# Splitting the product with v over three engines in a sparse graph attention kernel

## The chip, the cores and the metric

One core of a Trainium2 chip runs the kernel. The metric is the device time of one execution in microseconds (us), the median of several runs. Engines: PE is TensorE (PEld its weight loads), DVE is VectorE, ACT is ScalarE, POOL is GpSimd. SBUF is the core's working memory, PSUM the buffer that TensorE writes its results to. All runs compared here are in the fast state, and each kernel was timed beside runs of the kernel before on the same chip.

## The reference, cut to what matters

The task is one layer of graph attention with residuals and layer norms: 4096 nodes, 512 features, 8 heads of 64. The adjacency matrix is sparse, about 17 neighbours per node.

```python
q = (ht @ Wq + bq).reshape(T, H, HD) / sqrt(HD)
k = (hs @ Wk + bk).reshape(S, H, HD)
v = (hs @ Wv + bv).reshape(S, H, HD)
logits = einsum('thd,shd->hts', q, k)
logits = where(edge_mask[None] != 0, logits, NEG)
probs  = softmax(logits, axis=-1)
ctx    = einsum('hts,shd->thd', probs, v).reshape(T, D)
ht = layer_norm(ht + ctx @ Wo + bo)
out = _layernorm(x + ht + gelu(ht @ W1) @ W2)
```

## The kernel before: the parts that matter

The kernel makes lists of neighbours, projects k and v into a table in DRAM, and then treats targets in tiles of 128, sorted by their number of neighbours. Neighbours are called slots. GpSimd gathers the rows (k and v, 1024 floats) of three slots into one buffer. Six such buffers exist. VectorE multiplies k by q, reduces to logits, ScalarE exponentiates, VectorE multiplies v by the weights p, and TensorE transposes each product into one PSUM tile, where the transposes also sum over the slots. A feed-forward block (`pf`, `po`) is woven in between.

```python
def gather(dst, table, idx):
    nc.gpsimd.indirect_dma_start(out=dst, out_offset=None, in_=table[:, :], ...)   # L829

def values(i, j0, n, kv, p, cps, after):
    v4 = kv[:, :n, D:].rearrange("p j (h d) -> p j h d", h=H)
    nc.vector.tensor_tensor(v4, v4, p[:, j0:j0 + n, :].unsqueeze(3)                 # L942
                            .to_broadcast([P, n, H, HD]), ALU.mult)
    for j in range(n):
        for c in range(KC):
            nc.tensor.matmul(cps[:, c, :], kv[:, j, D + c * P:D + (c + 1) * P], ident,
                             is_transpose=True, ...)                                # L946
...
nc.vector.tensor_tensor(kv[:, :n, :D], kv[:, :n, :D],                               # L965
                        tq[:, :D].unsqueeze(1).to_broadcast([P, n, D]), ALU.mult)
nc.vector.tensor_reduce(lg[:, :n, :], ..., AX.X, ALU.add)                           # L969
nc.scalar.activation(p[:, j0:j0 + n, :], lg[:, :n, :], AF.Exp)                      # L973
...
if pend:
    values(*pend.pop())          # group k-1
    issue(k + AHEAD)             # three gathers, AHEAD = 4
```

`kv` and `tq` are in SBUF, `p` is in PSUM. The program order above is only a wish: a scheduler sets each engine's order when the program is built.

## Time and profile before

| | before |
|---|---|
| median (range) | 1908.8 us (1901.9 to 1910.5) |
| span of the profiled run | 1904.1 us |
| attention, first to last gather of k and v | 393 to 1766 us |
| TensorE, VectorE, ScalarE, GpSimd busy | 90, 84, 41, 50% |
| granted clock of TensorE | 0.970 |

The views are read in the prediction below: the busy table, the stretches, the groups by line, the queue of GpSimd. The shares are averages over stages.

### The profile page before, as it was taken

To read this page: it belongs to the slowest core of one execution; us is meant where nothing else is said; L and a number is where in the kernel's file an instruction comes from. 1 tells how busy PE (TensorE), PEld (TensorE's weight loads), DVE (VectorE), ACT (ScalarE), POOL (GpSimd) and SP (SyncE) were. 2 spreads that over 40 slices of the span, in tenths; PEclk is the share of its full clock that TensorE was granted. 3 is DMA by queue.
4 is the path that set the end of the run, shared out by engine and by line. 5 is a ranking of instruction groups with operands and counts; after the bars stand their busy time and mean duration, and the time that the engine had idled before them with its cause. 6 is when DMAs were issued, how large, how long until landed. Compare 5 with 4: busy or idle time off the path is not lost.

```text
span 1904.1 us, 21426 instructions
## 1 busy us (share of the span) xinstructions
PE 1722.6 (90%) x7282; PEld 1116.1 (59%) x7282; DVE 1597.0 (84%) x2845; ACT 772.7 (41%) x1234; POOL 958.0 (50%) x857
## 2 busy tenths in 40 slices
PE   6998889676889999997999999999999989899996
PEld 3443344333656666665676667666667666667664
DVE  5889987568999999998899899999999987788601
ACT  4666664432344455442343333343334333333310
POOL 1002332542544555566767676677766655556201
PEclk9999999898889999998999999999999999999998
DMA  8778875598988788876778787888888867677200
GB/s 288 253 242 269 284 261 190 182 359 307 381 293 290 263 287 285 284 239 200 252 258 302 238 315 262 311 270 301 298 292 290 276 224 259 212 252 256 81 1 24
DMA packets 145392, 482.34 MB, mean 253 GB/s; under 512 B 20292, under 2 KB 20856, under 8 KB 145272
## 3 DMA queue, kind: packets, MB, share of 16 engines
q0 software_dynamic: 99312, 356.83, 54.2%
q1 hardware_dynamic: 40256, 105.15, 16.7%
q10 hardware_dynamic: 5704, 18.89, 2.5%
q8 instruction: 60, 0.98, 0.2%
q14 instruction: 60, 0.49, 0.1%
HBM read 438.07 MB, written 42.73 MB: 253 GB/s over the span
## 4 chain that ended last, share of the span: by engine, by line
DVE 30%; PE 15%; DMA 12%; issue 9%; POOL 8%; ACT 1%; SPq 0%; DVEq 0%; POOLq 0%; ACTq 0%
DVE kv L965 9%; DMA kv<-kvd,rec 9%; DVE kv L942 7%; DVE lg L969 7%; PE po L1067 5%; POOL kv L829 5%; PE pf L1058 5%; PE cps L946 2%; PE t L899 2%; DMA w<-in_L_gnn_W_dram 2%; DVE cand L657 1%; DVE n_st L639 1%; DMA out_dram<-xt,rec 1%; DVE R L672 1%; POOL rec L729 1%
## 5 line engine op out<-in xcount | busy, mean ns | idle before, releaser
L829 POOL DMA_INDIRECT kv<-kvd,rec x600 | 707.3, 1179 | 382.4 <-PE cps L946 182.9
L1058 PE MATMUL pf<-h2T,w 128*128 128x256 f32 (+1 forms) x2176 | 475.0, 369 | 3.5 <-ACT h2T L926 2.9
L1067 PE MATMUL po<-w,gt 128*128 128x512 f32 x1024 | 468.6, 596 | 2.0 <-ACT gt L1061 2.0
L1058 PEld LDWEIGHTS pf<-h2T,w 128*128 128x128 f32 x2176 | 388.4, 192 | 73.5 <-issue 25.0
L965 DVE TENSOR_TENSOR kv<-kv,tq 128x1536 f32<-128x1536 f32 (+2 forms) x210 | 350.7, 1672 | 77.8 <-DMA kv<-kvd,rec 53.6
L942 DVE TENSOR_TENSOR kv<-kv,p 128x1536 f32<-128x1536 f32 (+2 forms) x210 | 349.4, 1667 | 3.5 <-ACT p L973 3.2
L969 DVE TENSOR_REDUCE lg<-kv 128x24 f32<-128x1536 f32 (+2 forms) x210 | 349.1, 1665 | 0.4
L946 PEld LDWEIGHTS cps<-ident,kv 128*128 128x128 f32 x2400 | 277.3, 143 | 91.4 <-DVE kv L942 45.7
L946 PE MATMUL cps<-ident,kv 128*128 128x128 f32 x2400 | 306.8, 277 | 24.5 <-DVE kv L942 23.6
L1067 PEld LDWEIGHTS po<-w,gt 128*128 128x128 f32 x1024 | 187.0, 192 | 184.0 <-issue 179.7
L629 POOL TENSOR_TENSOR n_rs<-n_ve,mhalf 128x2 f32<-128x2 f32 (+1 forms) x66 | 57.1, 865 | 330.0 <-DVE n_ve L622 290.1
L653 ACT ACTIVATE sg<-a 128x1024 uint8<-128x1024 int32 x128 | 135.1, 1056 | 184.6 <-DMA a<-in_adj_dram 118.5
L973 ACT ACT_TABLE_LOAD x83 | 106.5, 1283 | 164.7 <-DVE lg L969 142.0
L973 ACT ACTIVATE p<-lg 128x24 f32<-128x24 f32 (+2 forms) x178 | 34.3, 193 | 295.4 <-DVE lg L969 161.6
L1061 ACT ACTIVATE gt<-pf 128x512 f32<-128x512 f32 x128 | 76.5, 597 | 186.5 <-PE pf L1058 170.6
L899 PE MATMUL t<-wo,rb 128*128 128x512 f32 x256 | 124.7, 632 | 25.4 <-DVE rb L895 25.1
L1061 ACT ACT_TABLE_LOAD x110 | 141.1, 1283 | 2.0
L785 PE MATMUL pq<-wk,hT 128*128 128x512 f32 x256 | 118.9, 607 | 23.0 <-ACT row L787 18.7
L785 PE MATMUL pq<-wv,hT 128*128 128x512 f32 x256 | 116.9, 599 | 17.3 <-ACT row L787 8.7
L657 DVE MAX8 cand<-wd 128x8 uint16<-128x103 uint16 (+1 forms) x640 | 130.6, 251 | 0.7
L796 PE MATMUL pq<-wq,hT 128*128 128x512 f32 x256 | 118.3, 606 | 6.3 <-DVE row L799 4.5
L899 PEld LDWEIGHTS t<-wo,rb 128*128 128x128 f32 x256 | 49.8, 202 | 83.7 <-issue 52.3
(125 smaller groups left out, 1427.2 us busy)
## 6 DMA issues: line engine op xcount, KB each, us to landing
a<-in_adj_dram SPq DMA_DIRECT2D x128, 512.0 KB
kvd<-row ACTq DMA_DIRECT2D x32, 512.0 KB
kv<-kvd,rec POOLq DMA_INDIRECT x600
tq<-row SPq DMA_DIRECT2D x17, 512.0 KB
xin<-in_L_gnn_h_target_dram SPq DMA_DIRECT2D x16, 512.0 KB
w<-in_L_gnn_W_dram SPq DMA_DIRECT2D x8, 1024.0 KB
xin<-in_x_dram SPq DMA_DIRECT2D x15, 512.0 KB
tq<-row POOLq DMA_DIRECT2D x15, 512.0 KB
```

Of the source, the lines that this page charges most:

```text
L657: nc.vector.max(cand[:, h * SQ + s, :], wd[:, w0:w1])
L785: nc.tensor.matmul(pkv, hT[:, kc, j * P:(j + 1) * P], w[:, kc, :], start=kc == 0, stop=kc == KC - 1)
L829: nc.gpsimd.indirect_dma_start(out=dst, out_offset=None, in_=table[:, :], in_offset=bass.IndirectOffsetOnAxis(ap=idx, axis=0))
L899: nc.tensor.matmul(pa, ct[:, c, :], wo[:, c, :], start=c == 0, stop=c == KC - 1)
L942: nc.vector.tensor_tensor(v4, v4, p[:, j0:j0 + n, :].unsqueeze(3) .to_broadcast([P, n, H, HD]), ALU.mult)
L946: nc.tensor.matmul(cps[:, c, :], kv[:, j, D + c * P:D + (c + 1) * P], ident, is_transpose=True, start=j0 + j == 0 and c == 0, stop=j0 + j ...
L965: nc.vector.tensor_tensor(kv[:, :n, :D], kv[:, :n, :D], tq[:, :D].unsqueeze(1).to_broadcast([P, n, D]), ALU.mult)
L969: nc.vector.tensor_reduce(lg[:, :n, :], kv[:, :n, :D].rearrange("p j (h d) -> p j h d", h=H), AX.X, ALU.add)
L973: nc.scalar.activation(p[:, j0:j0 + n, :], lg[:, :n, :], AF.Exp)
L1058: nc.tensor.matmul(pf[:, k, :], w1[(f0 + k) // KC][:, kc, (f0 + k) % KC * P:((f0 + k) % KC + 1) * P], h2T[:, kc, :w], start=kc == 0, stop= ...
L1061: nc.scalar.activation(gt, pf, AF.Gelu_apprx_tanh)
L1067: nc.tensor.matmul(po[j], gt[:, k, j * P:(j + 1) * P], w2[(f0 + k) // KC][:, (f0 + k) % KC, :], start=False, stop=f0 + k == FC - 1, skip_g ...
```

## The change

The intent is to take work from the two fullest engines. In a group of three slots ScalarE makes the third product (eight products of 128x64, each with one weight per partition), so VectorE makes two. GpSimd adds the first two results, so TensorE transposes two results in place of three. Around this, a frame: gathers are issued earlier, the transposes are emitted one step later, the projections get a third PSUM buffer, and two flag tiles become 16-bit to make room.

```diff
-                        pkv = psi.tile([P, D], F32, name="pq", bufs=2)
+                        pkv = psi.tile([P, D], F32, name="pq", bufs=3)      # three places
...
+                    m = n - 1 if n == S else n
-                    v4 = kv[:, :n, D:]...; multiply by p[:, j0:j0 + n, :]
+                    v4 = kv[:, :m, D:]...; multiply by p[:, j0:j0 + m, :]
+                    slots = list(range(n))
+                    if m > 1:
+                        nc.gpsimd.tensor_add(kv[:, 0, D:], kv[:, 0, D:], kv[:, 1, D:])
+                        slots.remove(1)
+                    yield
-                    for j in range(n):
+                    for j in slots:            # transposes, as before
...
+                def by_scalar(kv, lg):
+                    pa = sp.tile([P, H], F32, name="pa")
+                    nc.scalar.activation(pa, lg[:, S - 1, :], AF.Exp)
+                    for hd in range(H):
+                        v = kv[:, S - 1, D + hd * HD:D + (hd + 1) * HD]
+                        nc.scalar.mul(v, v, pa[:, hd:hd + 1])
...
                             advance()
+                            if k:
+                                issue(k + AHEAD)
                             yield cost * n
                             if pend:
-                                values(*pend.pop())
-                                issue(k + AHEAD)
+                                tails.append(values(*pend.pop()))
...
+                            if n == S:
+                                by_scalar(kv, lg)
```

(Cut: the 16-bit flags, the closing condition of the transposes, the last call of `values`. "multiply by" stands for the `tensor_tensor` shown above. A *clump* below is a run of adds in GpSimd's queue with no gather between them.)

More of the change, by code (lines that the diff above doesn't have):

```diff
@@ L605, in late_constants @@
                 nc.vector.tensor_scalar_mul(bq8, bq8, HD ** -0.5)
-                pb = psi.tile([P, D], F32, name="pq", bufs=2)
+                pb = psi.tile([P, D], F32, name="pq", bufs=3)
                 for kc in range(KC):
@@ L674, in edges @@
                         nc.vector.match_replace(flat, top, flat, 0.0)
-                has = lp.tile([P, MAXE], F32, name="ehas")
+                has = lp.tile([P, MAXE], BF16, name="ehas")
                 nc.vector.tensor_scalar(has, rec[:, :MAXE], 0.0, 0.0, op0=ALU.is_gt,
@@ L793, in target @@
                     g, (t, hT) = order[n][1], state[n]
-                    pq = psi.tile([P, D], F32, name="pq", bufs=2)
+                    pq = psi.tile([P, D], F32, name="pq", bufs=3)
                     for kc in range(KC):
@@ L873, in finish @@
                 nc.vector.tensor_copy(degs[:, i:i + 1], rec[:, MAXE:MAXE + 1])
-                has = sp.tile([P, MAXE], F32, name="has", bufs=1)
+                has = sp.tile([P, MAXE], BF16, name="has", bufs=1)
                 nc.vector.tensor_scalar(has[:, :cap], rec[:, :cap], 0.0, None, op0=ALU.is_gt)
@@ L940, in values @@
                 def values(i, j0, n, kv, p, cps, after):
-                    v4 = kv[:, :n, D:].rearrange("p j (h d) -> p j h d", h=H)
-                    nc.vector.tensor_tensor(v4, v4, p[:, j0:j0 + n, :].unsqueeze(3)
-                                            .to_broadcast([P, n, H, HD]), ALU.mult)
-                    for j in range(n):
+                    m = n - 1 if n == S else n
+                    v4 = kv[:, :m, D:].rearrange("p j (h d) -> p j h d", h=H)
+                    nc.vector.tensor_tensor(v4, v4, p[:, j0:j0 + m, :].unsqueeze(3)
+                                            .to_broadcast([P, m, H, HD]), ALU.mult)
+                    slots = list(range(n))
[4 more added lines that the diff above has]
+                    for j in slots:
                         for c in range(KC):
@@ L947, in values @@
                                              is_transpose=True, start=j0 + j == 0 and c == 0,
-                                             stop=j0 + j == TILES[i][1] - 1, skip_group_check=True)
+                                             stop=j0 + n == TILES[i][1] and j == slots[-1],
+                                             skip_group_check=True)
                     if after is not None:
                         tails.append(after)
+                def by_scalar(kv, lg):
[4 more added lines that the diff above has]
+                        nc.scalar.mul(v, v, pa[:, hd:hd + 1])
                 for k in range(AHEAD + 1):
@@ L988, in attention @@
                             k += 1
-                values(*pend.pop())
+                tails.append(values(*pend.pop()))
                 while tails:
```

## The prediction

> **What bounds the kernel now.** I read the busy table and the slices first, then the groups by line and shape, then the waits, and last a table of stretches and the GpSimd queue in order of time.
>
> ```profile
> PE 1722.6 (90%) x7282; PEld 1116.1 (59%) x7282; DVE 1597.0 (84%) x2845; ACT 772.7 (41%) x1234; POOL 958.0 (50%) x857
> PE   6998889676889999997999999999999989899996
> DVE  5889987568999999998899899999999987788601
> ACT  4666664432344455442343333343334333333310
> POOL 1002332542544555566767676677766655556201
> ...
> DVE 30%; PE 15%; DMA 12%; issue 9%; POOL 8%; ACT 1%; SPq 0%; DVEq 0%; POOLq 0%; ACTq 0%
> ```
>
> Two engines share the bound, TensorE and VectorE: both are near full from slice 11 on, and the chain of waits jumps between them. ScalarE has more than half its time free. GpSimd looks half free, but that is an average: it is empty in the first eight slices and at 6 or 7 tenths in the middle. So I cut the run where the character changes (columns: PE, PEld, DVE, ACT, POOL busy us with counts, clock, DMA share, GB/s):
>
> ```profile
> 0.00:400.00 400.00, 339.10 (x929) 156.68 (x930) 309.84 (x1198) 226.01 (x413) 99.67 (x118) 0.98 0.74 248
> 400.00:900.00 500.00, 443.33 (x1967) 298.82 (x1966) 473.33 (x830) 207.16 (x324) 270.72 (x237) 0.94 0.81 290
> 900.00:1100.00 200.00, 190.80 (x904) 135.90 (x903) 179.12 (x175) 74.53 (x109) 136.38 (x115) 0.99 0.77 261
> 1100.00:1500.00 400.00, 380.66 (x1824) 269.92 (x1823) 380.71 (x341) 148.05 (x217) 288.73 (x242) 0.98 0.86 295
> 1500.00:1770.00 270.00, 254.58 (x1167) 178.16 (x1165) 223.23 (x218) 97.26 (x141) 151.16 (x135) 0.98 0.72 242
> ```
>
> Attention runs from 393 us (first gather of k and v) to 1766 us (last). At 1100 to 1500 us VectorE and TensorE are both at 95%. The groups that the change touches, in the whole run and in that stretch (busy us, mean ns, then idle before and its releasers):
>
> ```profile
> L829 POOL DMA_INDIRECT kv<-kvd,rec x600 | 707.3, 1179 | 382.4 <-PE cps L946 182.9 <-issue 150.8 <-DVE lg L969 14.4
> L942 DVE TENSOR_TENSOR kv<-kv,p 128x1536 f32<-128x1536 f32 x189 | 329.3, 1743 | 3.5 <-ACT p L973 3.2 <-issue 0.3
> L946 PE MATMUL cps<-ident,kv 128*128 128x128 f32 x2400 | 306.8, 277 | 24.5 <-DVE kv L942 23.6 <-issue 0.4
> ...
> L829 POOL DMA_INDIRECT kv<-kvd,rec x208 | 255.4, 1228 | 87.9 <-issue 53.1 <-PE cps L946 26.3 <-remote 3.0
> ```
>
> Each gather is followed by 0.30 us in which GpSimd waits for nothing that the profile shows. That is queue time, though not counted as busy. The gathers in order of time show it, with the first VectorE product, which has two SBUF inputs, beside them:
>
> ```profile
> 1206.39 0.94 POOL L829 DMA_INDIRECT kv<-kvd,rec  x1 [0.30 <-issue]
> 1207.63 0.94 POOL L829 DMA_INDIRECT kv<-kvd,rec  x1 [0.31 <-issue]
> 1208.87 2.20 POOL L829 DMA_INDIRECT kv<-kvd,rec  x1 [0.30 <-issue]
> ...
> 1208.51 1.75 DVE L965 TENSOR_TENSOR kv<-kv,tq 128x1536 f32<-128x1536 f32 x1
> ```
>
> A free gather takes 1.24 us from start to start. One that meets the product with q takes 2.20 us and ends as soon as that product has ended plus the usual time. Over all gathers, those that overlap this product average 1.59 us and the others 0.95 us.
>
> **What the Trainium skill says.** "SBUF — State Buffer", section "SBUF: two separate sides": VectorE with two SBUF inputs and GpSimd share a port pair as "an exclusive lock, not a bandwidth split". The gathers above behave so beside the product with q. The product with p does not hold gathers up (1.21 us against 1.16), and its second input lies in PSUM. The new add on GpSimd reads SBUF, so it can block, and be blocked by, the product with q.
>
> "GPSIMD Engine Reference", section 3.1 "Elementwise": an elementwise op with two tensors costs about twice what VectorE takes. The trace agrees. This kernel already runs 128x512 f32 products on GpSimd (1.27 us, undisturbed) and on VectorE (0.687 us).
>
> "ScalarE: Activation LUTs", section "What ACT_TABLE_LOAD costs": a table load takes about 1283 ns, and an activation some 186 ns + 0.833 ns per element, with 93 ns for each pointer operand, partly hidden back to back. The trace has 1283 ns loads and 194 ns for 128x24. With that page I estimate 0.24 us for one of the new 128x64 products, whose scale is a pointer.
>
> **The change part by part.** There are 210 groups of slots: 189 of three, 12 of two, 9 of one.
>
> VectorE: the product with p shrinks from 128x1536 (1743 ns) to 128x1024 (1208 ns, from the twelve groups of two): 189 x 0.535 = 101 us less.
>
> TensorE: 189 + 12 = 201 groups have one result less to transpose, so 201 x 4 = 804 transposes go. The mean of 277 ns is a modelled span of overlapping instructions. In order of time twelve of them cover 1.47 us, and eleven weight loads 1.23 us, so one costs 0.11 us of the queue: 88 us less.
>
> ScalarE: 189 x (one exponential 0.19 + 8 products x 0.24) = about 400 us more, from 773 to about 1170 us. It stays the least loaded engine, 66 to 70% in the stretch at 1100 us (37% + 17 groups per 100 us x 2.1 us). The built order has only six more table-load rows, counting both branches. The products start from the same logits as the exponential before them, so they run beside the next VectorE work. A gelu may wait up to 2 us behind them, which two buffers for its result mostly hide.
>
> GpSimd: 201 adds of 1.27 + 0.08 us (the gap seen between two such products) = 271 us more, plus what the lock costs: the product with q is on for 1.75 us of about 6.5 us per group, so every fourth add waits about 0.9 us, 0.2 us each. I use 1.55 us per add. The adds stand in the same queue as the gathers. In the built order they come in clumps of one to four, mostly three, after up to nine gathers, because six buffers allow that. Buffers are freed only after the add and its transposes.
>
> Third PSUM buffer for projections: before 450 us TensorE waits for ScalarE or VectorE to empty such a buffer for about 40 us. But the start of attention also hangs on the edge lists, on VectorE (91% at 100 to 300 us) and on the adjacency rows. I give it 8 us. The 16-bit flags make room in SBUF and are worth nothing here.
>
> Now the sum by stretch, with groups = gathers / 3 and queue time = busy + gaps of 0.3 us.
> - 0 to 400: -8 us.
> - 400 to 900, 63 groups: VectorE bound, saves 63 x 0.535 = 34; TensorE saves 63 x 0.44 = 28. GpSimd has 271 + 67 of 500 us; with 63 x 1.55 it comes to 436 and still fits. -28 us.
> - 900 to 1100, 30 groups: GpSimd 136 + 33 = 169, plus 46 = 215 in 200 us. +10 us, with some of the overrun met by lower lock time.
> - 1100 to 1500, 69 groups: 289 + 70 = 359, plus 107 = 466 us in 400. VectorE would need only 381 - 37 = 344, TensorE 381 - 30 = 351. GpSimd becomes the bound: +55 us, a little under the full 66 because a longer stretch meets fewer blocks.
> - 1500 to 1770, 37 groups: 151 + 40 + 57 = 248 of 270; TensorE could save 16. Two engines near full in lockstep: -8 us.
> - From 1770 on only the feed-forward runs: 0.
> The sum is +21 us on the 1909.5 us median: 1930 us. About 190 us of work leave the two bounding engines, and nearly all of the gain is spent on a new bound.
>
> **The rivals.** First, the plain reading: two engines share the bound, both lose about 5% of the run, and the helpers are free on average. Then 80 to 90 us go, and the time is near 1825 to 1850. For it speak the busy table and the idle time of GpSimd, much of which is a wait for the transposes that get fewer (183 us). Against it: in the stretch at 1100 us only 26 us of that wait are left in 400.
>
> Second, the clumps hurt more than the sum says. Until now a gather waited for TensorE alone. After the change GpSimd also stands still until VectorE has made the products, gathers behind it are late, and TensorE waits in order for the adds in front of feed-forward work. One more microsecond for each of 201 groups makes 2000 us or more. Six buffers and nine gathers per clump (11 to 14 us against about 15 us of VectorE work in three groups) speak against the worst.
>
> Third, ScalarE delays gelu and through it TensorE: at 70% load in one in-order queue I expect tens of short waits, 10 us in all.
>
> **Range and chances.** The first rival pulls down by up to 100 us and the second up by 70, so I take 1868 to 1995 us for 8 in 10. Within 2% means 1871 to 1948 us. Faster 0.22, same 0.46, slower 0.32.
>
> **What would show it.** Right: the VectorE product at about 1.2 us, transposes down to 1596, an add row on GpSimd with 201 entries of 1.3 to 1.6 us, and at the middle of attention GpSimd busy above 80% while VectorE and TensorE drop to 80 to 88%, with waits for gathers before the product with q well above today's 54 us. Groups would come every 6.5 us or slower there against 5.8 today. Wrong: if GpSimd shows room in the middle (gathers quicker than 1.2 us, or adds under 1 us), the first rival holds; if VectorE falls under 75% there, or TensorE waits long for the adds, the second.

## The result, and the profile after

The changed kernel takes 2038.6 us (2037.2 to 2046.7, 4 runs) against 1908.8 us. The ratio is 1.0696 (95% interval 1.0658 to 1.0735). A ratio here is the mean time of one kernel's fast runs over that of the other's in the same rounds, so it isn't quite the ratio of the medians. It is slower by 7%, above the range of the prediction.

The busy line of the changed kernel:

```profile
PE 1699.4 (83%) x6478; PEld 1068.1 (52%) x6478; DVE 1610.6 (79%) x2845; ACT 1177.8 (58%) x2941; POOL 1226.2 (60%) x1058
```

TensorE lost its 804 transposes, ScalarE and GpSimd took their new work as planned (1178 and 1226 us). But VectorE is *not* less busy: 1611 us against 1597, though its product with p shrank. The groups show where most of its saving went (busy us, mean ns, idle before and its releasers; by shape). First a line of the kernel before, then the changed kernel:

```profile
L965 DVE TENSOR_TENSOR kv<-kv,tq 128x1536 f32<-128x1536 f32 x189 | 330.2, 1748 | 74.8 <-DMA kv<-kvd,rec 50.7 <-PE pf L1058 12.2 <-DMA tq<-tq,rec 6.8
...
L981 DVE TENSOR_TENSOR kv<-kv,tq 128x1536 f32<-128x1536 f32 x189 | 390.9, 2069 | 169.2 <-DMA kv<-kvd,rec 148.9 <-issue 9.9 <-DMA tq<-tq,rec 4.8
...
L949 POOL TENSOR_TENSOR kv<-kv 128x512 f32<-128x512 f32 x201 | 263.8, 1327 | 111.1 <-DVE kv L945 108.2 <-DVE n_nm L634 0.4 <-issue 0.4
L945 DVE TENSOR_TENSOR kv<-kv,p 128x1024 f32<-128x1024 f32 x201 | 242.6, 1209 | 15.0 <-ACT p L989 12.9 <-ACT kv L966 1.3 <-issue 0.6
L954 PE MATMUL cps<-ident,kv 128*128 128x128 f32 x1596 | 235.3, 297 | 123.6 <-POOL kv L949 122.2
```

The product with p costs 1.21 us, as worked out. The product with q, which the change doesn't touch, went from 1748 to 2069 ns on the mean. And there are three new waits: GpSimd's add for VectorE's product (108 us), TensorE's transposes for the add (122 us), and VectorE for gathers (149 us here, 51 us before). Their sum isn't the loss, since they overlap and lie partly off the path.

One place in order of time shows the first of these. The queue of GpSimd, then VectorE:

```profile
1316.46 3.73 POOL L949 TENSOR_TENSOR kv<-kv 128x512 f32<-128x512 f32 x3
...
1317.55 4.26 DVE L981 TENSOR_TENSOR kv<-kv,tq 128x1536 f32<-128x1536 f32 x1
```

Three adds run back to back to 1320.19 us. The product with q starts among them and ends at 1321.81, which is 1.62 us after the last add: about its whole time alone. It stood still through the clump. I compared start and end of every product of 128x1536 with every add in the trace: the 57 that overlapped an add averaged 2.81 us (4.73 us the longest), the 132 others 1.75 us. That is 57 x 1.06 = 60 us of VectorE standing, recorded as busy, and the same as the difference of the two lines above (390.9 - 330.2).

The product with q is not all. VectorE's other instructions that overlap an add took 35 us longer in sum than their medians in no_add (a run below, without the add), the smaller products with q 5 us. For example, a product of 16-bit tiles, `wd`, took 1.08 us where it overlapped an add (11 times) and 0.45 us elsewhere; `xt`, normalised in place, took 1.80 us (7 times) and 0.54 us elsewhere. So VectorE stands for about 100 us, as much as it was to save.

The stretches (columns as in the prediction):

```profile
400.00:900.00 500.00, 408.14 (x1676) 269.70 (x1676) 460.55 (x815) 319.12 (x812) 338.33 (x280) 0.90 0.80 283
900.00:1100.00 200.00, 167.40 (x667) 112.03 (x666) 159.03 (x155) 119.80 (x329) 154.69 (x134) 0.90 0.66 226
1100.00:1500.00 400.00, 326.23 (x1342) 224.00 (x1340) 331.38 (x288) 247.43 (x684) 312.89 (x256) 0.91 0.70 243
```

In the middle TensorE is at 82% and VectorE at 83%: no engine is full by this view. GpSimd comes nearest, at 78% busy plus some 13% of gaps. The windows do not hold the same work in both kernels, so I also timed the same gathers, counted from 1 to 600, from start to start (single rows move by up to 10 us if the count is shifted by one, since gathers come in bursts):

| work (gathers of k and v) | before | after | difference | predicted |
|---|---|---|---|---|
| until the first | 393 us | 394 us | +1 | -8 |
| 1 to 194 (ends at 900 us before) | 507.5 | 532.6 | +25 | -28 |
| 194 to 283 (1100) | 200.3 | 215.5 | +15 | +10 |
| 283 to 490 (1500) | 399.6 | 483.9 | +84 | +55 |
| 490 to the last (1766) | 265.2 | 271.2 | +6 | -8 |

The loss is everywhere in attention, and largest where GpSimd is fullest.

### The profile page after: what moved, and what is told of

It is laid out like the page before. It is cut to its first block, busy times and chain, and to the rows that moved or that the text cites. A ratio compares the mean times of both kernels' runs of the same rounds, so it can differ in the third digit from the quotient of the medians.

```text
span 2036.5 us, 22105 instructions
## 1 busy us (share of the span) xinstructions
PE 1699.4 (83%) x6478; PEld 1068.1 (52%) x6478; DVE 1610.6 (79%) x2845; ACT 1177.8 (58%) x2941; POOL 1226.2 (60%) x1058
## 5 line engine op out<-in xcount | busy, mean ns | idle before, releaser
L829 POOL DMA_INDIRECT kv<-kvd,rec x600 | 690.9, 1151 | 248.8 <-issue 170.0
L981 DVE TENSOR_TENSOR kv<-kv,tq 128x1536 f32<-128x1536 f32 (+2 forms) x210 | 416.4, 1983 | 180.5 <-DMA kv<-kvd,rec 160.2
L1086 PE MATMUL po<-w,gt 128*128 128x512 f32 x1024 | 480.1, 607 | 6.0 <-ACT gt L1080 5.6
L1077 PEld LDWEIGHTS pf<-h2T,w 128*128 128x128 f32 x2176 | 397.1, 195 | 78.1 <-issue 29.6
L966 ACT ACTIVATE kv<-kv,pa 128x64 f32<-128x64 f32 x1512 | 389.4, 335 | 10.4 <-issue 0.4
L954 PE MATMUL cps<-ident,kv 128*128 128x128 f32 x1596 | 235.3, 297 | 123.6 <-POOL kv L949 122.2
L949 POOL TENSOR_TENSOR kv<-kv 128x512 f32<-128x512 f32 x201 | 263.8, 1327 | 111.1 <-DVE kv L945 108.2
L954 PEld LDWEIGHTS cps<-ident,kv 128*128 128x128 f32 x1596 | 202.7, 153 | 186.5 <-POOL kv L949 154.2
L945 DVE TENSOR_TENSOR kv<-kv,p 128x1024 f32<-128x1024 f32 (+1 forms) x210 | 248.5, 1186 | 15.0 <-ACT p L989 12.9
L899 PE MATMUL t<-wo,rb 128*128 128x512 f32 x256 | 136.3, 682 | 48.2 <-DVE rb L895 48.2
```

Of the source, the lines that this page charges most:

```text
L899: nc.tensor.matmul(pa, ct[:, c, :], wo[:, c, :], start=c == 0, stop=c == KC - 1)
L945: nc.vector.tensor_tensor(v4, v4, p[:, j0:j0 + m, :].unsqueeze(3) .to_broadcast([P, m, H, HD]), ALU.mult)
L949: nc.gpsimd.tensor_add(kv[:, 0, D:], kv[:, 0, D:], kv[:, 1, D:])
L966: nc.scalar.mul(v, v, pa[:, hd:hd + 1])
L981: nc.vector.tensor_tensor(kv[:, :n, :D], kv[:, :n, :D], tq[:, :D].unsqueeze(1).to_broadcast([P, n, D]), ALU.mult)
L1077: nc.tensor.matmul(pf[:, k, :], w1[(f0 + k) // KC][:, kc, (f0 + k) % KC * P:((f0 + k) % KC + 1) * P], h2T[:, kc, :w], start=kc == 0, stop= ...
```

## The experiments

My theories when I began: *queue length* (GpSimd has too much to do per group, the main step of the prediction), *coupling* (VectorE, GpSimd and TensorE wait for each other in fixed order), *port lock* (the add and the product with q exclude each other), and *ScalarE* (its products delay others). Twelve kernels ran, each in 3 timed rounds.

| run | what | median us | ratio to before |
|---|---|---|---|
| change | all | 2038.6 | 1.0696 |
| no_add | without the add | 1942.2 | 1.0167 |
| frame | frame only | 1925.0 | 1.0079 |
| add_early | add on finished data | 2004.3 | 1.0494 |
| spread_add | add behind the newest gathers | 2174.0 | 1.1399 |
| no_scalar | without ScalarE's product | 2057.6 | 1.0754 |
| add_vec | add on VectorE | 1910.5 | 1.0000 |
| set_early | fill on finished data | 1895.2 | 0.9915 |
| spread_early | add ahead of its step's gathers | 1994.6 | 1.0434 |
| set_late | fill in the add's place | 1962.8 | 1.0273 |
| se_set | spread_early with a fill | 1915.1 | 1.0042 |
| third_buf | third PSUM buffer alone | 1905.7 | 0.9992 |
| vec_old | add on VectorE, old frame | 1903.2 | 0.9976 |

**1. Take parts away: no_add, no_scalar, frame, third_buf.**

```diff
 no_add
-                    if m > 1:
-                        nc.gpsimd.tensor_add(kv[:, 0, D:], kv[:, 0, D:], kv[:, 1, D:])
-                        slots.remove(1)
 no_scalar
-                    m = n - 1 if n == S else n
+                    m = n
-                            if n == S:
-                                by_scalar(kv, lg)
 frame: both;  third_buf: the kernel before with bufs=3 for "pq"
```

> The changed kernel without the add on GpSimd: ScalarE still takes the third product, VectorE the other two, TensorE transposes all three results again (2400 transposes). If the add on GpSimd is the whole cost (by its queue time, its order or the shared port), the time falls below the kernel before, to 1850 to 1900 us, since VectorE keeps its 101 us of saving and GpSimd is as free as before. If the ScalarE products (390 us of them) or the new program frame are a large part of the loss, it stays above 1960 us.

> The changed kernel without ScalarE's product: VectorE makes all three products, GpSimd still adds two results, TensorE transposes two. If the add on GpSimd is the main cost, 2000 to 2070 us, as slow as the whole change. If ScalarE's 390 us of products are a main cost, it falls below 1980 us.

> Only the frame of the change: third PSUM buffer, 16-bit flags, gathers issued earlier, transposes emitted one step later; VectorE makes all three products, no add, no ScalarE product. All theories: within 1.5% of the kernel before (1880 to 1935 us), by the third buffer perhaps 8 us faster. If it is above 1950 us, the frame itself costs and the others are to be read anew.

> The kernel before with the third PSUM buffer for projections alone. I predicted 8 us of gain from it: 1895 to 1908 us. If it is the part of the frame that costs (frame 1925 us): 1918 to 1930 us.

Without the add 96 us of the 130 are gone; without ScalarE's product none. So the add is the main cost and ScalarE isn't. But no_add missed my figure by 42 us: it is slower than the kernel before, and 17 us slower than the frame alone, although VectorE is busy far less. Its busy line:

```profile
PE 1736.5 (89%) x7282; PEld 1134.0 (58%) x7282; DVE 1507.9 (78%) x2845; ACT 1176.5 (61%) x2941; POOL 935.4 (48%) x857
```

VectorE fell by 89 us and the time did not fall. TensorE still has its 7282 operations. So moving a third of VectorE's product to ScalarE bought nothing here by itself; why it costs 17 us on top of the frame stays open. The frame costs 16 us. Its third buffer alone made no difference (1905.7 us): that leaves the new order of emission and the 16-bit flags, which I did not part.

**2. The same queue time without the waits: add_early.** The add works on the halves with k times q, which are done a group earlier and which TensorE doesn't read. Its output is wrong, which doesn't matter for the time.

```diff
-                        nc.gpsimd.tensor_add(kv[:, 0, D:], kv[:, 0, D:], kv[:, 1, D:])
+                        nc.gpsimd.tensor_add(kv[:, 0, :D], kv[:, 0, :D], kv[:, 1, :D])
```

> Wrong result on purpose: the same add of the same size on GpSimd, but on the halves that hold k times q, which are finished a group earlier and which TensorE does not read. Queue time, port lock and release of buffers stay; the waits of the add for the product with p and of the transposes for the add go. Theory of coupling (waits in order between VectorE, GpSimd and TensorE): falls by more than 80 us, to 1900 to 1955 us. Theory of queue length (GpSimd simply has too much to do per group): stays at 2000 to 2040 us. Theory of the port lock alone: stays as well.

It fell by 34 us only. At 2004.3 us it lies at the edge of what queue length and lock had been given (2000 to 2040 us) and far from the figure of the coupling (1900 to 1955): the waits between product, add and transposes are a part, but most of the loss is still there.

**3. The same queue time without reading SBUF: set_early and set_late.** GpSimd fills 1359 floats with zero in place of the add. That takes 1.25 us and only writes. In set_early it stands where add_early's add stood, in set_late where the change's add stood, with the same waits. Their outputs are wrong, which doesn't matter for the times.

```diff
 set_early
+                        nc.gpsimd.memset(kv[:, :n, :453 if n == S else D], 0.0)
 set_late
+                        nc.gpsimd.memset(kv.rearrange("p j d -> p (j d)")[:, D:D + (1359 if n == S else 2 * D)], 0.0)
```

> Wrong result on purpose, as add_early, but in place of the add GpSimd fills 1359 elements with zero, which takes about the same 1.27 us (from the fills at the start of the program) and reads nothing from SBUF. Against add_early at 2004 us: theory of the port lock between an add that reads SBUF and the product with q: the product goes back from 2.01 us to about 1.75 us and the time falls by 40 to 60 us, to 1945 to 1965 us. Theory of queue time: within 15 us of 2004 us.

> Wrong result on purpose: the fill of 1359 zeros (1.25 us, reads nothing from SBUF) stands exactly where the add stood, on the two slots that it joined, so it waits for the product with p and the transposes wait for it. Only the reading of SBUF is gone. Theory of the port lock: 1900 to 1945 us, against 2039 us with the add. Theory of queue time or of waits in order: above 2000 us.

set_early is 109 us faster than add_early, about twice the gain that I expected of the lock, and even 0.85% faster than the kernel before. set_late is 76 us faster than the change and 18 us above my range for the lock. The groups in add_early, then in set_early:

```profile
L981 DVE TENSOR_TENSOR kv<-kv,tq 128x1536 f32<-128x1536 f32 x189 | 380.3, 2012 | 136.2 <-DMA kv<-kvd,rec 116.0 <-PE pf L1077 9.2 <-DMA tq<-tq,rec 4.5
L949 POOL TENSOR_TENSOR kv<-kv 128x512 f32<-128x512 f32 x201 | 271.4, 1365 | 76.7 <-DVE lg L985 74.4 <-DVE n_nm L634 0.3
```

```profile
L981 DVE TENSOR_TENSOR kv<-kv,tq 128x1536 f32<-128x1536 f32 x189 | 331.1, 1752 | 61.0 <-DMA kv<-kvd,rec 45.4 <-DMA tq<-tq,rec 6.2 <-PE pf L1077 3.5
L949 POOL MEMSET kv<- 128x1359 f32 x189 | 232.8, 1252 | 34.4 <-DVE lg L985 34.3
L949 POOL MEMSET kv<- 128x1024 f32 x12 | 11.6, 970 | 0.0
```

The product with q is back at 1.75 us, whether it overlaps a fill (55 products, 1.753 us) or not (134, 1.752 us); in add_early the 46 that overlapped an add took 2.83 us, up to 5.95. With it the wait for gathers before that product falls from 116 to 45 us. GpSimd's busy time for adds or fills differs by only 27 us (271.4 against 232.8 + 11.6), less than the 109. So most of it is the lock, not the queue.

A fill holds VectorE up too. VectorE's instructions other than the product with q that overlap a fill took 43 us longer in sum than their medians in no_add: `xt` 1.94 us (7 times) against 0.57 us, while `wd` is not held (0.45 and 0.46 us). So these pairs measure the reading of SBUF, and not all that VectorE and GpSimd do to each other.

There was one flaw: the order of clumps in GpSimd's queue differs between fill and add in both pairs (add_early has 6 clumps of three and 7 of four, set_early one of each).

**4. Hold the order fixed: spread_add, spread_early, se_set.** An ordering edge puts each add behind the newest group of gathers (spread_add), or behind the group before and ahead of its own step's gathers (spread_early). In both, the queue alternates three gathers and one add. se_set is spread_early with the fill.

```diff
 spread_add
-                        nc.gpsimd.tensor_add(...)
+                        with tc.issue_after(newest[0].ins):      # last gather issued
+                            nc.gpsimd.tensor_add(...)
 spread_early: besides, issue(k + AHEAD) moves behind values(...), and
+                    with tc.issue_after(newest[1].ins):          # last add
+                        newest[0] = gather(...)
 se_set: spread_early with set_late's fill as the add
```

> The changed kernel with one ordering edge: each add is queued behind the newest gather of its own program step, so that GpSimd's queue alternates three gathers, one add, in place of clumps of two to four adds. All work is the same. Theory of coupling by clumps: the waits of GpSimd for the product with p (108 us) mostly go, time 1930 to 1990 us. Theory of queue length: within 20 us of 2039 us.

> As spread_add, three gathers and one add in turn, but each add stands one group of gathers earlier, in front of the gathers of its own step. In spread_add each add was stuck behind gathers that wait for a buffer which the add before it had to set free: a loop without slack. Theory of that loop: 1990 to 2060 us, far below 2174 us. If alternation as such is bad: above 2120 us.

> Wrong result on purpose: spread_early with the same fill in place of the add, so that GpSimd's queue is held to the same fixed alternation of gathers and fills in both, and a different order of clumps can't be the reason. Port lock: falls by 60 us or more from 1995 us, to 1890 to 1935 us, and the product with q from 2.11 us to about 1.75 us. If the gain of set_early came from its other order: within 20 us of 1995 us.

spread_add was a clear miss: I expected a gain and it lost 135 us more, with GpSimd's wait for the product almost gone as planned. Its waits (us in total, times, longest):

```profile
PEld cps L955 <- POOL kv L950: 384.4, 172, 11.0
DVE kv L982 <- DMA kv<-kvd,rec: 288.7, 133, 5.2
PE cps L955 <- POOL kv L950: 286.4, 144, 10.8
...
POOL kv L829 <- PE cps L955: 171.6, 76, 7.0
```

TensorE waits for adds at 144 places, and gathers wait for transposes. The add stands behind gathers that need the buffer which the add before it has to set free through TensorE: a ring without slack over six buffers. Moved ahead by one group of gathers, the same work takes 179 us less (spread_early, 1994.6 us, the best order that I found with the add on GpSimd). The clumps of the change lie between these two, so the change's order is not the worst one, which is what I had thought.

With the alternation held the same, the fill in place of the add gains 79 us (1994.6 to 1915.1), and the product with q goes from 2.11 to 1.75 us:

```profile
L983 DVE TENSOR_TENSOR kv<-kv,tq 128x1536 f32<-128x1536 f32 x189 | 398.0, 2106 | 141.4 <-DMA kv<-kvd,rec 124.7 <-issue 6.2 <-PE cps L956 5.2
```

```profile
L983 DVE TENSOR_TENSOR kv<-kv,tq 128x1536 f32<-128x1536 f32 x189 | 331.3, 1753 | 125.4 <-DMA kv<-kvd,rec 89.1 <-PE cps L956 13.2 <-issue 8.4
```

Of the 79 us, 67 are the standing of this product itself (398.0 - 331.3). The granted clock of TensorE is the same in both (0.937 and 0.935). The other engines' orders were still the scheduler's, and the fill is about 0.1 us shorter than the add (1.25 against 1.37 us, some of which is the lock again). Three pairs now agree on 76 to 109 us for an add that reads SBUF.

**5. Take the add off GpSimd: add_vec, vec_old.** `nc.vector.tensor_add` in place of `nc.gpsimd.tensor_add`, in the new frame and in the frame of the kernel before.

> The add moves from GpSimd to VectorE (201 adds of about 0.69 us, so VectorE does some 37 us more than in the kernel before); TensorE keeps its 804 transposes less; GpSimd is as free as before. If it is GpSimd's queue that costs, 1880 to 1935 us. If any further step between the product and the transposes costs, wherever it runs, above 1960 us.

> In the frame of the kernel before (two PSUM buffers, gathers issued behind the product, transposes with it): ScalarE takes the third product, VectorE the other two and their add, TensorE transposes two. add_vec without the new frame. If the frame costs 16 us here as well, 1885 to 1900 us, which would beat both kernels; if the split of work gains nothing, 1905 to 1925 us.

add_vec is as fast as the kernel before, 128 us faster than the change, although VectorE does 136 us of adds. vec_old is 1903.2 us, between its two expected ranges, ratio 0.9976 with interval 0.9934 to 1.0018: no proven gain. So the rearrangement is worth nothing with the add on VectorE, the one form with fewer transposes, a right result and no add on GpSimd that I ran; the fastest correct kernels here (vec_old, third_buf, before) can't be told apart.

## Why the prediction was wrong

**Most parts were sized right.** The product with p at 1.21 us, 1596 transposes, 201 adds at 1.33 us (1.3 to 1.6 predicted), ScalarE at 1178 us (1170; its 1512 products cover 389.4 us, 0.26 us each, where the estimate from the skill's page was 0.24), TensorE and VectorE at 82 and 83% in the middle (80 to 88). GpSimd was at 78% there, just under the sign of "above 80%".

**The step that failed** is the cost of the lock in "The change part by part": "every fourth add waits about 0.9 us, 0.2 us each". I had seen the lock and named it, but counted only one side, the add that waits for the product. The other side is dearer: the product with q, on one of the two fullest engines, stands still for the add, and through a whole clump of adds. Instead of 201 x 0.2 = 40 us on GpSimd the runs show 76 us (set_late), 79 us (se_set) and 109 us (set_early) of time for the same edit, reading SBUF or not. Directly it is 60 us of VectorE standing in the product with q, and 40 us in its smaller forms and in other instructions, which the prediction did not have at all; the rest is argued, not shown: VectorE's delay makes the next add, transposes and gathers late. With the reading alone taken out (set_late, 1963 us) the time is inside the predicted range, 33 us above its figure.

**The queue step was partly right.** GpSimd did become full: in set_early, where the product with q isn't held and most waits are gone, busy time plus gaps fill about 97% of GpSimd between 900 and 1500 us. The same gathers 283 to 490 take 435.4 us there against 399.6 before: +36 us, where I had put +55. That the queue causes this is not shown: in add_vec, without any add in GpSimd's queue, the same gathers take 429.7 us, +30 (there VectorE has the adds). And the queue alone isn't the loss, for set_early as a whole beats the kernel before.

**The light stretches.** I booked 36 us of gain in the first and the last stretch of attention by comparing loads with the length of each stretch. Set against the table above, -28 and -8 became +25 and +6. set_early shows what was there without most of the lock and the waits: 11, 4 and 22 us gained in the three stretches beside the middle. A sum of loads that "still fits" isn't yet a time when three engines wait for each other in order.

**The rivals.** The second rival (clumps and waits) was real and had too little weight: 34 us (add_early against the change) to 68 us (set_early against set_late). With the lock it carries the time to where it is. The first rival, the plain reading, found no support: VectorE's 89 us less gave nothing (no_add), and with both engines relieved and no reading of SBUF 14 us were gained (set_early), not 80 to 90, though GpSimd's fills take queue time there. The third, ScalarE, isn't the cause of the loss: without it the kernel is 19 us slower still.

**The third buffer**, -8 us, was 0 (third_buf: 1905.7 against 1908.7 us, interval of the ratio 0.9966 to 1.0018).

**Slips in the working** that did not decide it: GpSimd isn't empty in the first eight slices but 25% busy (99.67 of 400 us); 37% + 17 x 2.1% is 73% for ScalarE, not 66 to 70 (62% was measured); the first rival's 80 to 90 us lead to 1820 to 1830, not 1825 to 1850 us; the result of gelu has three buffers in the kernel, not two; a held gather ends 0.8 us after the product, a little less than the whole 0.94 us of a free one; and 1909.5 us is one run, the median is 1908.8.

A ledger from the medians, along one path of edits: before 1909; frame +16; ScalarE's product +17 (no_add less frame); fewer transposes, paid with a fill's queue time, -47 (set_early less no_add); reading SBUF +109 (add_early less set_early); waits in order +34 (change less add_early): 2038. By the other path, over set_late, the waits are 68 and the reading 76. Each edit is built in its own order by the scheduler, so single terms carry an error of about the 34 us by which the two paths differ. The granted clock of TensorE was lower after (0.922 against 0.970); in add_vec and set_early it was 0.940 too, and their times are at or below the time before, so I don't read it as the cause.

## What to carry to other kernels

Before work moves to GpSimd, look at which VectorE instructions read two SBUF operands and run at the same time: count the lock from both sides, and for the fuller engine first, and count clumps as one hold. In this trace those products were the larger part of the standing (65 us), other VectorE instructions the rest (35 us), so look at the durations of all of them. An engine that looks half idle may be the one on which all others wait in order, so ask for each new instruction what stands behind it in the queue and which buffer it sets free. Where a queue's order is the scheduler's, test it with a twin of the instruction that takes the same time and reads nothing before believing that order or load is the reason.

## What the Trainium skill lacked or had wrong

- "SBUF — State Buffer", section "SBUF: two separate sides" holds, the exception that GpSimd must read SBUF included: products that overlap an add take 2.81 us, those that overlap a fill 1.753 us, alone 1.75 us. What it lacks is what happens to a queue: a waiting VectorE product did not get the ports between two adds, and stood to the end of a clump of three (4.26 us; in add_early 5.95 us the longest).
- The same page, section "Who interferes with whom", reports a probe in which `tensor_tensor` did not stall a DMA. The indirect gathers here, which read their row numbers from SBUF, are held up by one with two SBUF inputs: 1.59 us where they overlap the product with q by more than 0.1 us, 0.95 us elsewhere. The page doesn't say what the probe's DMA read, so this is a gap of the page rather than a contradiction. Why the gather is held, no run here shows.
- "GPSIMD Engine Reference", section 3.1 "Elementwise", gives times for adds, and names no time for a fill on GpSimd: here 0.97 us for 128x1024 and 1.25 us for 128x1359.
